# The last batch's second shared product moved behind the routed tiles, and the conditional tiles behind all

## The chip, the cores and the metric

The kernel runs on one core of one Trainium2 chip. The metric is the device time of one execution in microseconds (us). Times in the profile count from the first instruction of the span. The engines are called as in the profile: PE (TensorE, the matmuls) with its weight loads PEld, DVE (VectorE), ACT (ScalarE), POOL (GpSimd) and SP (SyncE, which here only issues transfers). A "q" behind an engine's name is its sequencer.

## The reference

Eight batches of 256 rows of 512 numbers (2048 rows, float32) pass through cross-attention and then a mixture of experts, each with a residual:

```python
x = x + xattn(layernorm(x), ctx, ctx)            # 32 heads of 16, 8 key/value groups, then @ Wfc.T + bfc
h = layernorm(x)
scores = softmax(h @ gate_weight.T)              # 8 experts
topk_w, topk_i = group_limited_topk(scores)      # 2 of 8 experts for each row
e = einsum(silu(h @ gate_w) * (h @ up_w), down_w)        # each expert, width 352
routed = sum over the two chosen experts of e * topk_w
shared = (silu(h @ sh_gate_w.T) * (h @ sh_up_w.T)) @ sh_down_w.T   # width 704, every row
x = x + routed + shared
```

The change touches `shared` of the last batch, in its second product, the one with `sh_down_w`.

## The kernel before, in words

The kernel has two parts. In the attention part PE goes through the 64 units of attention, and a planner (`Others`, with `Stage` objects that have a cost, a start and a due time) fills the gaps between them with the other work of each batch `b`: projections, `close(b)` (the product with Wfc, the residual in `acc`, the second layernorm), `router(b)` (the choice of experts, and the scattering of each row into a table `rows` in device memory, ordered by expert, with an indirect transfer from POOL) and `feed.pieces(b)` of the class `Shared`. `pieces(b)` is a generator. It makes first the products `gu` with the shared gate and up weights (L173) and from them `act`, then the second product `o` with the shared down weights (L193), one group of six products for each half (`q`) of the batch. DVE adds `acc` to it (L202) and SP writes the sum to `out` (L204). Every yielded piece is reckoned at 0.88 by the planner; `Shared.TOTAL` is their sum.

When attention is over, the pieces of the last batch (7) are handed as `tail` to `routed`. On PE the tail lies between attention and the routed tiles. The instruction order on PE, ACT, DVE and SP is that of the program text. SP's order at the handover is: weights of expert 0 (`up_weights`, `down_weights`, L365 and L368), rows of tiles 0 to 2 (`load`, L386), weights of experts 1 and 2, eight transfers `rows<-blank` which clear the ends of the experts' parts of the table (L536), the tail's two writes of `out`, and then what `run` issues. The tail is stepped to 0.8 of its cost, then tile 0 is transposed (`turn(0)`), then the tail is stepped to its end.

In the routed part a tile is 128 rows for one expert (or twice 64 rows for two experts, a "half" tile). 35 tiles are run: the first tile of each of the 8 experts, 24 further ones, and 3 half tiles at positions 12, 19 and 26. `run` is a software pipeline. In iteration `n` it issues the load of the rows of tile `n+2` and, at the start, the weights of the expert three tiles ahead, so the rows of tile 3 stand on SP behind the weights of expert 3. PE then does `turn` of tile `n+1` (four transpositions, `rx`, L397, copied by ACT), `up` of tile `n` (16 products `rg`, L429), `down` of tile `n-1` (6 products `ro`, L460) and `turn_act` of tile `n` (`ra`, L452). The result of `down` is weighted by DVE (`ry`, L471) and added to its rows of `out` in device memory by an indirect transfer of POOL that accumulates (L474). Each of these waits for the one before, since all write `out`. `last` does the last tile in smaller steps.

The second experts' weights of the half tiles are loaded into two tiles of their own, `wgu_2` and `wd_2` (`second`, L390 and L391).

How many tiles are needed depends on the data. `plan` works it out on the chip (`t_all`), and what the 35 tiles can't hold is done by `more`: every engine loads the value (L557) and branches (`tc.If`, L563). With these inputs nothing more is needed, so all engines only take the branch. `more` is called in iteration `MORE_AT`, 27.

Of the kernel before, what the change touches and what calls it, by code (L numbers as in the profile page):

```python
# [43 lines left out]
F32 = mybir.dt.float32  # L44
# [6 lines left out]
P = 128  # L51
# [20 lines left out]
N_HALF = N_EXP // 2  # L72
RUN_FULL, RUN_HALF = 24, 3
N_PLAN = N_FULL + N_HALF
MORE_AT = 27
W = 528
W_ID = D + N_EXP
EPS = 1e-5
# [6 lines left out]
@with_exitstack  # L85
def xattn_ffn(
    ctx: ExitStack,
    tc: tile.TileContext,
    x: bass.AP,
    ctxT: bass.AP,  # L90
    wq: bass.AP,
    wkv: bass.AP,
    wfc: bass.AP,
    bfc: bass.AP,
    wgate: bass.AP,
    wsg: bass.AP,
    wsd: bass.AP,
    wgu: bass.AP,
    wd: bass.AP,
    out: bass.AP,  # L100
):
    nc = tc.nc

    ctx.enter_context(tc.manual_schedule(engines={ENG.PE, ENG.Activation, ENG.DVE, ENG.SP}))

    keep = ctx.enter_context(tc.tile_pool(name="keep", bufs=1))
    dram = ctx.enter_context(tc.tile_pool(name="dram", bufs=1, space=bass.MemoryType.DRAM))
    ps_m = ctx.enter_context(tc.tile_pool(name="ps_m", bufs=3, space=PSUM))
    right = ctx.enter_context(ExitStack())
    left = ctx.enter_context(ExitStack())  # L110

    ident = keep.tile([P, P], F32, name="ident")
    make_identity(nc, ident)


    t_exp = keep.tile([P, N_PLAN], I32, name="t_exp")
    t_row = keep.tile([P, N_PLAN], I32, name="t_row")
    t_one = keep.tile([P, N_PLAN, N_EXP], F32, name="t_one")
    t_all = keep.tile([P, 1], I32, name="t_all")

    t_end = keep.tile([P, N_EXP], I32, name="t_end")

    blank = dram.tile([R, W], F32, name="blank")
    rows = dram.tile([N_EXP * S_R + P, W], F32, name="rows")

    feed = Shared(right, tc, ps_m, wsg, wsd, out)
    tail = attention(
        left, tc, ps_m, feed, x, ctxT, wq, wkv, wfc, bfc, wgate, out, ident,
        rows, t_exp, t_row, t_one, t_all, t_end, blank,
    )  # L130
    left.close()
    routed(ctx, tc, ps_m, wgu, wd, ident, rows, t_exp, t_row, t_one, t_all, t_end, blank, out, tail, right)


class Shared:


    TOTAL = (11 + 2 * 3) * 2 * 0.88

    def __init__(self, ph, tc, ps_m, wsg, wsd, out):  # L140
        self.nc, self.ps_m, self.wsg, self.wsd, self.out = tc.nc, ps_m, wsg, wsd, out
        wp = ph.enter_context(tc.tile_pool(name="wsh", bufs=1, side="right"))
        self.sums = ph.enter_context(tc.tile_pool(name="sums", bufs=2, side="right"))
        act = ph.enter_context(tc.tile_pool(name="act", bufs=1, side="right"))
        self.work = ph.enter_context(tc.tile_pool(name="sg", bufs=2, side="right"))

        self.gu = {
            k: wp.tile([P, NC, 2 * n if n == P else P], F32, name=f"gu_w{k}") for k, n in SCH
        }
        self.down = wp.tile([P, len(SCH), D], F32, name="down")  # L150
        self.hT, self.acc = {}, {}

        self.act = act.tile([P, len(SCH), S], F32, name="act")
        self.nc.gpsimd.memset(self.act[SCH[0][1] :, SCH[0][0]], 0.0)
# [10 lines left out]
    def pieces(self, b):  # L165
        nc, ps_m = self.nc, self.ps_m
        hT = self.hT.pop(b)
        act = self.act
        for k, n in SCH:
            ps = ps_m.tile([P, 2, S], F32, tag="m", name=f"gu{b}_{k}")  # L170
            for i in range(2 if n == P else 1):
                for c in range(NC):
                    nc.tensor.matmul(  # L173
                        ps[:, i],
                        lhsT=self.gu[k][:, c, i * P : (i + 1) * P],
                        rhs=hT[:, c],
                        start=(c == 0),
                        stop=(c == NC - 1),
                    )
                    if c == 1 or (c == NC - 1 and i == 0 and n == P):  # L180
                        yield 0.88, True, 0
            gate, up = ps[:n, 0], ps[:, 1] if n == P else ps[n:, 0]

            sg = self.work.tile([P, S], F32, tag="sg", name=f"sg{b}_{k}")
            nc.scalar.activation(sg[:n], gate, AF.Tanh, scale=0.5)
            nc.vector.scalar_tensor_tensor(sg[:n], sg[:n], 1.0, gate, ALU.add, ALU.mult)
            nc.vector.scalar_tensor_tensor(act[:n, k], sg[:n], 0.5, up, ALU.mult, ALU.mult)
            yield 0.88, False, 0
        acc = self.acc.pop(b)
        for q in range(QC):  # L190
            ps = ps_m.tile([P, D], F32, tag="m", name=f"o{b}_{q}")
            for i, (k, n) in enumerate(SCH):
                nc.tensor.matmul(  # L193
                    ps,
                    lhsT=act[:, k, q * P : (q + 1) * P],
                    rhs=self.down[:, k],
                    start=(i == 0),
                    stop=(i == len(SCH) - 1),
                )
                if i < len(SCH) - 1:  # L200
                    yield 0.88, True, 0
            nc.vector.tensor_add(acc[q], ps, acc[q])  # L202
            t0 = (b * QC + q) * P
            nc.sync.dma_start(self.out[t0 : t0 + P, :], acc[q])  # L204
            yield 0.88, False, 0
# [133 lines left out]
    tc.add_to_no_dep_group("rows", dma)  # L339


def routed(ctx, tc, ps_m, wgu, wd, ident, rows, t_exp, t_row, t_one, t_all, t_end, blank, out, tail, right):

# [34 lines left out]
    def load(i):  # L380
# [3 lines left out]
        for p in range(0, P, step):  # L384
            first = i * S_R if k < 0 else value(t_row, k, ENG.SP, N_EXP * S_R, p)
            nc.sync.dma_start(xs[i][p : p + step], rows[bass.ds(first, step), :])  # L386

    def second(i):
        e = value(t_exp, i - N_EXP, ENG.SP, N_EXP - 1, R)
        nc.sync.dma_start(wgu_2, wgu[bass.ds(e, 1)].rearrange("o p c f -> p (o c) f"))  # L390
        nc.sync.dma_start(wd_2, wd[bass.ds(e, 1)].rearrange("o p c d -> p (o c) d"))  # L391

    def turn(i):
# [12 lines left out]
            nc.vector.tensor_mul(wt, row[:, D : D + N_EXP], t_one[:, i - N_EXP])  # L406
            nc.vector.tensor_reduce(w1s[i], wt, AX.X, ALU.add)
        ids[i] = []
        for part, _ in halves(i, None, None):
            to = place(early, [P, 1], f"id{part.start}", f"rid{i}_{part.start}", 6, I32)  # L410
            to = to[: part.stop - part.start]
            nc.vector.tensor_copy(to, row[part, W_ID : W_ID + 1].bitcast(I32))
            ids[i].append(to)

    def halves(i, w, w_2):

        if i < N_EXP + N_FULL:
            return [(slice(0, P), w)]
        return [(slice(0, R), w), (slice(R, P), w_2)]

    def of_expert(i):
        exps[i] = i if i < N_EXP else value(t_exp, i - N_EXP, ENG.PE, N_EXP - 1)
# [1 line left out]
    def product(dst, i, cols):  # L424

        for c in range(NC):
            w = wgu_all[:, bass.ds(exps[i], 1), c, cols].rearrange("p o f -> p (o f)")
            for part, w in halves(i, w, wgu_2[:, c, cols]):
                nc.tensor.matmul(  # L429
                    dst[part],  # L430
                    lhsT=xTs[i][:, c, part],
                    rhs=w,
                    start=(c == 0),
                    stop=(c == NC - 1),
                )
# [20 lines left out]

    def down_chunk(o, i, fc, fn):
        w = wd_all[:fn, bass.ds(exps[i], 1), fc].rearrange("p o d -> p (o d)")
        for part, w in halves(i, w, wd_2[:fn, fc]):
            nc.tensor.matmul(  # L460
                o[part],
                lhsT=aTs[i][:fn, fc, part],
# [5 lines left out]
    def add_up(o, i):  # L468
# [1 line left out]
        y = place(work, [P, D], "y", f"ry{i}", 3)  # L470
        nc.vector.tensor_scalar(y, o, w1s.pop(i), None, ALU.mult)  # L471

        for to, (part, _) in zip(ids.pop(i), halves(i, None, None)):
            nc.gpsimd.indirect_dma_start(  # L474
                out=out,
                out_offset=bass.IndirectOffsetOnAxis(ap=to, axis=0),
# [57 lines left out]
    for e in range(N_EXP):  # L534
        to = value(t_end, e, ENG.SP, N_EXP * S_R)
        alone(tc, nc.sync.dma_start(rows[bass.ds(to, R), :], blank).ins)  # L536
    while tail.cost < 0.8 * tail.total:
        tail.step()
    turn(0)
    while not tail.over:  # L540
# [5 lines left out]
    others = ctx.enter_context(  # L546
        tc.tile_pool(name="others", bufs=1, side="right", reuse_waits="tile")
    )

    wgu_2 = others.tile([P, NC, 2 * F], F32, name="wgu_2")  # L550
    wd_2 = others.tile([P, len(FCH), D], F32, name="wd_2")

    def more():

        nonlocal spare
# [18 lines left out]
    def run(tiles):  # L574

        halfs = [n for n, i in enumerate(tiles) if i >= N_EXP + N_FULL]
        seconds = [0 if len(tiles) < N_EXP else N_EXP - 3, *(n + 3 for n in halfs)]
        for n, i in enumerate(tiles):
            if 3 <= n + 2 < len(tiles):
                load(tiles[n + 2])  # L580
            if i + 3 < N_EXP:
                up_weights(i + 3)
                down_weights(i + 3)
            for k, at in zip(halfs, seconds):
                if at == n:
                    second(tiles[k])
            if n + 1 == len(tiles):
                last(i, tiles[n - 1])
                break
            turn(tiles[n + 1])  # L590
            up(i)
            if n > 0:
                down(tiles[n - 1])
            turn_act(i)
            if n == MORE_AT:
                more()

    full = [N_EXP + k for k in range(N_FULL)]
    half = [N_EXP + N_FULL + k for k in range(N_HALF)]
# [6 lines left out]
def attention(  # L606
# [368 lines left out]
    def close(b):  # L975
# [7 lines left out]
        for qc in range(QC):  # L983
            ps = ps_m.tile([P, D], F32, tag="m", name=f"fc{b}_{qc}")
            for c in range(NC):
# [7 lines left out]
                if c < NC - 1:  # L993
                    yield 0.88, True, 0
            nc.vector.tensor_add(acc[qc], ps, acc[qc])
            moments(mv, acc[qc], qc, f"f{b}")
            if qc == 0:
                yield 0.88, False, 0
# [284 lines left out]
    def closed(b):  # L1283
        end = UNITS * (b + 1)
        if b + DEEP in gates:
# [11 lines left out]
            )  # L1297
        )
        shared.append(
            others.add(feed.pieces(b), feed.TOTAL, end + 6, end + 16.5, cl, *shared[-1:])  # L1300
        )

    def transfers():
# [122 lines left out]
```

## Time and profile before

| | |
|---|---|
| median of 3 runs | 945.8 us (943.48 to 947.02) |
| the profiled execution | 944.63 us, of which 942.9 us are the span from the first to the last instruction |
| PE busy | 923.3 us (98%) |
| DVE, ACT, POOL busy | 454.4, 202.7, 134.1 us |
| PE's granted clock over the span | 0.997 |
| shared second products `o` (L193), 8 batches | 192 instructions, 90.3 us busy |
| routed up products `rg` (L429) | 552 instructions, 169.3 us busy |
| SP's queue | 66.43 MB, 21.9% of 16 DMA engines' span |
| POOL's queue of indirect transfers | 17.83 MB, 8.9% |

A float32 product shows as two matmul instructions. The start of a group in the timeline is the start of its first instruction; the ends of matmuls are modelled and overlap the next start, so that the time of a group on PE is read from one start to the next. The table of 40 slices has one digit for each 23.6 us. The handover from attention to the routed tiles lies in slices 27 and 28.

### The profile page before, as it was taken

To read this page: it belongs to the slowest core of one execution; us is meant where nothing else is said; L and a number is where in the kernel's file an instruction comes from. 1 tells how busy PE (TensorE), PEld (TensorE's weight loads), DVE (VectorE), ACT (ScalarE), POOL (GpSimd) and SP (SyncE) were. 2 spreads that over 40 slices of the span, in tenths; PEclk is the share of its full clock that TensorE was granted. 3 is DMA by queue.
4 is the path that set the end of the run, shared out by engine and by line. 5 is a ranking of instruction groups with operands and counts; after the bars stand their busy time and mean duration, and the time that the engine had idled before them with its cause. 6 is when DMAs were issued, how large, how long until landed. Compare 5 with 4: busy or idle time off the path is not lost. (4 is left out here: it accounts for less than half of the span.)

```text
span 942.9 us, 12985 instructions
## 1 busy us (share of the span) xinstructions
PE 923.3 (98%) x5005; PEld 545.0 (58%) x5005; DVE 454.4 (48%) x1028; ACT 202.7 (21%) x257; POOL 134.1 (14%) x171
## 2 busy tenths in 40 slices
PE   9999999999999999999999999999999999999995
PEld 8775566546445555664654645785566555564563
DVE  4554857466756766554775645371222222222222
ACT  1224123323222232222232231101111111111110
POOL 4000100201101101100121021020121121121211
PEclk9999999999999999999999999999999999999998
DMA  6367610201102111002011011079963353533322
GB/s 223 84 199 227 172 36 2 83 6 34 47 13 81 47 24 46 27 27 45 24 47 46 1 48 45 23 273 382 396 162 73 83 147 63 149 69 68 68 34 34
DMA packets 37904, 86.23 MB, mean 91 GB/s; under 512 B 6289, under 2 KB 14737, under 8 KB 35921
## 3 DMA queue, kind: packets, MB, share of 16 engines
q1 hardware_dynamic: 29152, 66.43, 21.9%
q0 software_dynamic: 7648, 17.83, 8.9%
q10 hardware_dynamic: 1040, 1.12, 0.4%
q8 instruction: 42, 0.69, 0.3%
q14 instruction: 22, 0.17, 0.1%
HBM read 54.99 MB, written 25.93 MB: 86 GB/s over the span
## 5 line engine op out<-in xcount | busy, mean ns | idle before, releaser
L904 DVE TENSOR_REDUCE nm<-s 128x8 f32<-128x2048 f32 x64 | 146.5, 2289 | 86.5 <-PE s L895 82.3
L429 PE MATMUL rg<-wgu_all,rxT 128*128 (+2 forms) x552 | 169.3, 460 | 0.0
L936 ACT ACTIVATE ex<-s 128x2048 f32<-128x2048 f32 x64 | 120.1, 1877 | 225.8 <-PE s L928 216.1
L173 PE MATMUL gu<-hT,gu_w 128*128 128x256 f32 x704 | 166.6, 385 | 0.0
L173 PEld LDWEIGHTS gu<-hT,gu_w 128*128 128x128 f32 x704 | 129.1, 190 | 41.0 <-issue 24.6
L429 PEld LDWEIGHTS rg<-wgu_all,rxT 128*128 128x128 f32 (+1 forms) x552 | 99.6, 185 | 53.6 <-issue 6.9
L460 PE MATMUL ro<-wd_all,raT 128*128 (+5 forms) x210 | 96.5, 594 | 0.0
L474 POOL DMA_INDIRECT y<-ry,rid x38 | 58.4, 1537 | 253.3 <-DVE ry L471 140.7
L193 PE MATMUL o<-down,act 128*128 128x512 f32 x192 | 90.3, 603 | 0.3 <-DVE q L334 0.3
L446 DVE TENSOR_TENSOR ract<-rg,rsg 128x352 f32<-128x352 f32 x34 | 17.8, 524 | 139.6 <-PE rg L429 139.6
L928 PE MATMUL s<-qT,kT 17*128 17x512 f32 x512 | 73.0, 640 | 2.0 <-DVE nm L904 1.9
L895 PE MATMUL s<-kT,qT 16*128 16x256 f32 x1024 | 73.4, 400 | 1.5 <-ACT ex L936 0.8
L895 PEld LDWEIGHTS s<-kT,qT 16*128 16x128 f32 x1024 | 46.3, 184 | 30.9 <-ACT ex L936 14.1
L460 PEld LDWEIGHTS ro<-wd_all,raT 128*128 128x128 f32 (+3 forms) x210 | 38.4, 186 | 42.9 <-issue 36.2
L861 PE MATMUL pq<-xT,wq_sb 128*128 128x256 f32 x256 | 61.2, 386 | 0.5 <-DVE acc L202 0.3
L947 PE MATMUL av<-ex,v 128*32 128x512 f32 x512 | 61.5, 598 | 0.0
L986 PE MATMUL fc<-wfc_sb,o 128*128 128x512 f32 x128 | 60.9, 603 | 0.1
L471 DVE TENSOR_SCALAR ry<-ro,rw 128x512 f32<-128x512 f32 x35 | 26.3, 750 | 71.9 <-PE ro L460 71.9
L399 ACT COPY rxT<-rx 128x512 f32<-128x512 f32 x35 | 20.5, 585 | 187.4 <-PE rx L397 187.4
L1111 POOL DMA_INDIRECT rows<-lnf,idx x32 | 31.6, 988 | 200.6 <-DVE idx L1105 189.7
L193 PEld LDWEIGHTS o<-down,act 128*128 128x128 f32 x192 | 33.9, 190 | 40.6 <-issue 39.3
L861 PEld LDWEIGHTS pq<-xT,wq_sb 128*128 128x128 f32 x256 | 46.6, 190 | 14.5 <-issue 6.0
(183 smaller groups left out, 723.6 us busy)
## 6 DMA issues: line engine op xcount, KB each, us to landing
wgu_all<-wgu SPq DMA_DIRECT2D x8, 1408.0 KB
xs<-rows SPq DMA_DIRECT2D x32, 264.0 KB
wd_all<-wd SPq DMA_DIRECT2D x8, 768.0 KB
wgu<-wgu SPq DMA_DIRECT2D x3, 1408.0 KB
cT<-ctxT SPq DMA_DIRECT2D x8, 512.0 KB
acc<-x SPq DMA_DIRECT2D x16, 256.0 KB
y<-acc SPq DMA_DIRECT2D x16, 256.0 KB
x<-x SPq DMA_DIRECT2D x14, 256.0 KB
```

The lines of the kernel that those rows point to most:

```text
L173: nc.tensor.matmul(ps[:, i], lhsT=self.gu[k][:, c, i * P : (i + 1) * P], rhs=hT[:, c], start=(c == 0), stop=(c == NC - 1),)
L193: nc.tensor.matmul(ps, lhsT=act[:, k, q * P : (q + 1) * P], rhs=self.down[:, k], start=(i == 0), stop=(i == len(SCH) - 1),)
L429: nc.tensor.matmul(dst[part], lhsT=xTs[i][:, c, part], rhs=w, start=(c == 0), stop=(c == NC - 1),)
L460: nc.tensor.matmul(o[part], lhsT=aTs[i][:fn, fc, part], rhs=w, start=(fc == 0), stop=(fc == len(FCH) - 1),)
L474: nc.gpsimd.indirect_dma_start(out=out, out_offset=bass.IndirectOffsetOnAxis(ap=to, axis=0), in_=y[part], in_offset=None, compute_op=ALU.add,)
L861: nc.tensor.matmul(ps[:, i], lhsT=wq_sb[:, c, part], rhs=xT[:, c], start=(c == 0), stop=(c == NC - 1),)
L895: nc.tensor.matmul(ps[:, r, j], lhsT=qT[band, G, j0 + j, qc * P : (qc + 1) * P], rhs=kT[band, G], start=True, stop=True,)
L904: nc.vector.tensor_reduce(nms[b, G, j0][:, qc], ps, AX.X, ALU.max, negate=True)
L928: nc.tensor.matmul(ps[:, r], lhsT=kT[band, G, kc * P : (kc + 1) * P], rhs=qT[band, G, j0 : j0 + 2], start=True, stop=True,)
L936: nc.scalar.activation(ex, ps, AF.Exp, scale=HD**-0.5)
L947: nc.tensor.matmul(av[32 * r : 32 * r + 32], lhsT=vs[b % DEEP][:, kc, 4 * G + r], rhs=ex[:, r], start=(kc == 0), stop=(kc == QC - 1),)
L986: nc.tensor.matmul(ps, lhsT=o[:, c, qc * P : (qc + 1) * P], rhs=wfc_sb[:, c], start=(c == 0), stop=(c == NC - 1),)
```

## The change

`pieces` of the last batch ends after the first product. `act` is written to a new table `kept` in device memory by SP, in the place where the tail's two writes of `out` stood. `close` of the last batch writes `acc` (input plus attention) to `out` at once. After the last tile the two halves of batch 7 are read back from `out`, which by then has the routed parts added, the second product is made from `kept` and the down weights (both loaded again in iteration 28, into the buffer of the half tiles' second weights, which becomes one tile `two`), added to them, and written. `more` comes behind that. The tail stops two pieces before its end for `turn(0)`, and in iteration 0 `turn(1)` stands behind `up(0)` instead of before it.

```diff
 class Shared:
-    TOTAL = (11 + 2 * 3) * 2 * 0.88
+    UP = 11 * 2 * 0.88
+    TOTAL = UP + 2 * 3 * 2 * 0.88
...
             yield 0.88, False, 0
+        if b == B - 1:
+            nc.sync.dma_start(self.kept, act)
+            return
         acc = self.acc.pop(b)
...
+    def two(a, m, b, n):
+        t = others.tile([P, len(SCH) * (D + S)], F32, tag="two", name="two")
+        return (
+            t[:, : a * m].rearrange("p (a m) -> p a m", m=m),
+            t[:, a * m : a * m + b * n].rearrange("p (b n) -> p b n", n=n),
+        )
...
     def second(i):
         e = value(t_exp, i - N_EXP, ENG.SP, N_EXP - 1, R)
+        seconds[i] = wgu_2, wd_2 = two(NC, 2 * F, len(FCH), D)
...
-    while tail.cost < 0.8 * tail.total:
+    while tail.cost < tail.total - 2 * 0.88:
         tail.step()
     turn(0)
...
-            turn(tiles[n + 1])
+            if n == halfs[-1] + 2:
+                down_sh, act_sh = two(len(SCH), D, len(SCH), S)
+                nc.sync.dma_start(down_sh, wsd)
+                nc.sync.dma_start(act_sh, kept)
+            if n > 0:
+                turn(tiles[n + 1])
             up(i)
             if n > 0:
                 down(tiles[n - 1])
+            else:
+                turn(tiles[n + 1])
             turn_act(i)
-            if n == MORE_AT:
-                more()
+
+        sums = []
+        for q in range(QC):
+            t0 = ((B - 1) * QC + q) * P
+            to = out[t0 : t0 + P, :]
+            sums.append((to, work.tile([P, D], F32, tag=f"sum{q}", bufs=1, name=f"sum{q}")))
+            nc.sync.dma_start(sums[q][1], to)
+        for q, (to, y) in enumerate(sums):
+            ps = ps_m.tile([P, D], F32, tag="m", name=f"o{B - 1}_{q}")
+            for i in range(len(SCH)):
+                nc.tensor.matmul(
+                    ps,
+                    lhsT=act_sh[:, i, q * P : (q + 1) * P],
+                    rhs=down_sh[:, i],
+                    start=(i == 0),
+                    stop=(i == len(SCH) - 1),
+                )
+            nc.vector.tensor_add(y, ps, y)
+            nc.sync.dma_start(to, y)
+        more()
...
             nc.vector.tensor_add(acc[qc], ps, acc[qc])
+            if b == B - 1:
+                nc.sync.dma_start(out[(b * QC + qc) * P : (b * QC + qc + 1) * P, :], acc[qc])
             moments(mv, acc[qc], qc, f"f{b}")
...
-            others.add(feed.pieces(b), feed.TOTAL, end + 6, end + 16.5, cl, *shared[-1:])
+            others.add(
+                feed.pieces(b), feed.UP if b == B - 1 else feed.TOTAL, end + 6, end + 16.5, cl, *shared[-1:]
+            )
```

## The prediction

> **What bounds the kernel now.** I read the page first, then four answers of the trace: the chain of waits, TensorE's (PE's) waits, the timeline around the handover from the attention part to the routed part, and the timeline of the start and the end. The page says that PE is busy nearly throughout:
>
> ```profile
> span 942.9 us, 12985 instructions
> PE 923.3 (98%) x5005; PEld 545.0 (58%) x5005; DVE 454.4 (48%) x1028; ACT 202.7 (21%) x257; POOL 134.1 (14%) x171
> DMA  6367610201102111002011011079963353533322
> ```
>
> So moving PE work changes the time only by what it leaves uncovered. The DMA row shows one place where PE isn't alone: slices 27 to 29 (about 613 to 684 us) are the loading of the routed weights. By windows:
>
> ```profile
> 628.00:649.00 21.00, 21.00 (x74) 13.02 (x73) 5.22 (x20) 3.68 (x6) 0.00 (x0) 1.00 0.92 360
> 649.00:659.00 10.00, 9.31 (x35) 5.39 (x33) 1.98 (x7) 1.05 (x2) 0.00 (x0) 1.00 1.00 386
> ```
>
> The last three columns are granted clock, DMA share and GB/s: PE and the DMA engines are full at the same time. Here the change takes PE work away and takes hardly a byte from the DMA. The sync queue's (SP's) issues in that stretch, and PE's timeline:
>
> ```profile
> 634.85 11.61 SPq L536 DMA_DIRECT2D rows<-blank  x8
> 646.55 1.00 SPq L204 DMA_DIRECT2D y<-acc  x2
> 647.61 0.45 SPq L365 DMA_DIRECT2D wgu_all<-wgu  x1
> 648.10 0.43 SPq L368 DMA_DIRECT2D wd_all<-wd  x1
> 648.78 0.33 SPq L386 DMA_DIRECT2D xs<-rows  x1
> ```
> ```profile
> 633.71 5.31 PE L193 MATMUL o<-down,act 128*128 128x512 f32 x12
> 638.86 0.60 PE L397 MATMUL rx<-ident,xs 128*128 128x128 f32 x4
> 639.30 5.32 PE L193 MATMUL o<-down,act 128*128 128x512 f32 x12
> 658.61 0.49 PE L452 MATMUL ra<-ident,ract 128*128 128x128 f32 x3
> 659.16 0.63 PE L397 MATMUL rx<-ident,xs 128*128 128x128 f32 x4
> ```
>
> The last line is the transposition of tile 3. Its rows are the `xs<-rows` load issued at 648.78; that load's sixteen completion increments arrive from 656.09 to 659.02, 0.14 us before PE starts on it. Before the change PE meets this load just as it lands. That is the centre of my prediction.
>
> **Part 1: the second product leaves the handover.** Two groups of 12 instructions, 5.15 us each by the starts above (633.71 to 638.86), so PE is 10.3 us earlier if nothing stops it. Follow it: the first product ends at 633.9; tile 0's rows land at 632.85, so its transposition, now two pieces earlier, starts at 633.0 instead of 632.1; with the rest of the pieces the first product ends at 635.1. Then `up(0)` 4.73, transposition of tile 1 0.44, 0.25 for the activation (the wait was 0.69, and the swapped transposition, 0.44, now lies in it), `turn_act` 0.38, tile 2 0.44, `up(1)` 4.73, `down(0)` 2.58, `turn_act` 0.38: PE stands before tile 3 at 649.0, ten microseconds early. Tiles 1 and 2 (landed by 634.7) and the weights of experts 0 to 2 (landed by 645.9, expert 1's by 640.7) don't stop it.
>
> Tile 3's load can't come earlier. On SP it stands behind the eight `blank` transfers and expert 3's weights, in the new program too, and the queue moves its bytes in order: from 628 us 768 + 3x264 + 2x2176 + 8x132 + 512 + 2176 + 264 = 9920 KB. The change takes out the 512 KB of `y<-acc` (now sent when `close` has added, when the DMA is nearly idle) and puts in `kept<-act`, 768 KB. The page gives that queue 21.9% of the span for 66.43 MB, 3.1 us per MB: 0.26 MB more is +0.8 us. Tile 0's scatter-add, formerly issued at 659.84 and so behind this load, is now issued near 650; its queue takes 8.9% for 17.83 MB, 4.7 us per MB, so its 0.26 MB costs up to 1.2 us of the same engines. Bounds for tile 3's landing: 656.1 (all sixteen parts as the earliest) plus 0.8, up to 659.02 + 0.8 + 1.2. I take 659.9, nearest to the measured landing with half of these additions, so PE starts tile 3 at 660.05 against 659.16: **+0.9 us** (range -2.0 to +2.0). The 10.3 us removed are a wait of 11 us. Behind it nothing is late: tile 4's rows landed at 664.96, and PE wants them 8 us after tile 3.
>
> **Part 2: the clock after that wait.** The trace has both ends of such a pause (timeline of the start, then the windows of the end):
>
> ```profile
> 1.81 4.45 PE L1217 MATMUL warm<-ident 128*128 128x128 f32 x20 [1.81 <-POOL ident masks.py:199]
> 7.83 1.95 PE L805 MATMUL pkv<-wkv_sb,cT 128*128 128x128 f32 x16
> ```
> ```profile
> 938.00:943.00 5.00, 0.00 (x0) 0.00 (x0) 0.00 (x0) 0.00 (x0) 0.00 (x0) 0.50 0.11 20
> ```
>
> Twenty products of 128 columns take 4.45 us at the start, later sixteen take 1.95: 0.22 against 0.11 us each, so PE runs at half speed for its first 4.2 us. And after its last matmul (932.6) the granted clock falls to 0.50 (at 937.8, 5.2 us later). A pause of 11 us therefore costs half of about 4.2 us: **+2.1 us**, between 1.7 and 3.4 for where the change of clock falls.
>
> The Trainium skill ("TensorE: Matmul & The Clock Gate", "What's actually happening") speaks against the change at this place: it has the array halve its clock after an idle window of about 3.4 us and regain it after as long a busy one. By that the price would be an estimated 1.7 us in place of 2.1, and a wait of 4 us would already pay it, which no row here shows.
>
> **Part 3: the conditional tiles leave tile 27.**
>
> ```profile
> PE rx L397 <- PEq L563: 1.9, 1, 1.9
> ```
>
> PE waits once for its branch, 1.9 us with nothing beside it; the path is PE's from there to the end. **-1.9 us.** At the new place the branch lies behind all of PE's work; its cost belongs to the end.
>
> **Part 4: small things.** `act_sh` and `down_sh` are 2.3 MB on SP at iteration 28, about 6 us at 386 GB/s; the next `xs` load queues behind them and is wanted two iterations (16 us) later: nothing. If that cover were gone, up to 6 us. The wait of `kept<-act` on SP holds up expert 3's weights and tile 3's load behind it, but `act` is done near 636.5 and SP gets there at 646.5: nothing. The one tile for both second weights changes no order. The early writes of batch 7's `acc` make SP wait near 584, but its next instruction waits for batch 6 until 608 anyway: nothing.
>
> **Part 5: the end.** Now:
>
> ```profile
> 932.65 0.75 DVE L471 TENSOR_SCALAR ry<-ro,rw 128x512 f32<-128x512 f32 x1 [1.44 <-PE ro L460]
> 934.56 1.55 POOL L474 DMA_INDIRECT y<-ry,rid  x1 [4.03 <-DMA y<-ry,rid]
> ```
> ```profile
> 934.34 1.77 POOLq L1422
> ```
>
> PE ends at 932.6, the last scatter-add lands at 939.17, and the program ends 3.7 us later: 0.8 for SP's closing waits, then GpSimd's (POOL's) drain until 942.1, then 0.8 of handshake. After the change (same clock face) PE goes on with the product: 2x5.15 = 10.3 us, to 942.9. Meanwhile SP waits for the scatter, reads the rows back from 939.25 (`acc<-x`, the same size, took 2.8 us to land: 942.05, the second half 942.6), so the read is hidden, with 0.3 us to spare; behind SP's wait for it stand only the two writes. POOL, which has its own branch behind the last scatter, waits there for its landing and then 1.4 us (the `INC_SWDGE_SEM` of L563), to 940.7, and holds up nobody. Last come the addition, 0.69 (the `acc<-o,acc` form), the write, 2.1 (`y<-acc` at 608.36 and 616.32 landed after 2.02 and 2.16), 0.2 of the branch's semaphores on SP, 0.8 of closing and 0.8 of handshake, POOL's drain being over by then: 942.9 + 0.15 + 0.69 + 0.1 + 2.1 + 0.2 + 1.6 = 947.7, against 942.9: **+4.8 us**. Bounds: 4.5 without the branch, 6.9 if the drain follows the landing as it does now. So the product is not free behind the tiles: of its 10.3 us, 5.5 fall into time in which PE was already done.
>
> **Sum.** +0.9 + 2.1 - 1.9 + 4.8 = +5.9 us. The profiled execution took 944.63 us (942.9 of span and 1.7 around it), so it becomes 950.5. It lay 1.2 us below the median of the three runs; from the median: 951.7 us.
>
> **Rivals.** (a) *The freed PE time is kept* (faster). If tile 3's rows were in place by 649.0, PE would gain the ten microseconds and no clock would fall: -10.0 - 1.9 + 4.8 = -7.1, 938.7 us. It decides by one thing: each microsecond that tile 3's load lands before 659.0 is one gained, and the change is even where it lands at about 656 with the clock up, or 654 with it down. For it speaks that PE is 98% busy; against it the DMA share of 0.92 and 1.00 and the 9920 KB ahead of the load. Chance 0.05. (b) *The load lands early within its own spread* (no change). The sixteen parts lay 2.9 us apart; if the slowest engine doesn't lag in the new order, tile 3 starts at about 657.3: -1.9 + 1.9 - 1.9 + 4.8 = +2.9, 948.7 us. The spread of expert 1's load was 1.6, so a lag of 2.9 isn't the rule. Chance 0.27. (c) *A worse end*, drain and read-back included: +6.9 instead of 4.8, 953.8 us; counted with the forecast.
>
> **How the numbers follow.** The forecast, rows of tile 3 waited for, clock halved, end exposed, has 0.68. About 0.5% (4.7 us) is what a measurement of this kernel can tell from no change; +5.9 is over it, +2.9 within it. Low end: -2.0 + 1.7 - 1.9 + 4.5 = +2.3, or 948.1, opened to 947.5 for a shorter end; high end: +2.0 + 3.4 - 1.9 + 6.9 = +10.4, or 956.2.
>
> **What would show it.** Right: no `o` matmul before tile 0; PE idle for about 10 us before the transposition of tile 3, released by `xs<-rows`; matmuls at twice their spacing for some 4 us behind it; `rx(4)` some 3 us later than 667.3; no wait on L563 among the tiles; PE's last matmul about 10 us after the last tile's, and the span's end some 5 us behind that. Wrong: tile 3 transposed near 650, or the read-back landing after the product.

## The result, and the profile after

The changed kernel took 952.8 us (median of 5 runs, 951.49 to 954.48) against 946.97 us (5 runs) of the kernel before, run beside it: a ratio of 1.0068 with a 95% interval of 1.0046 to 1.0091, or +6.4 us (4.4 to 8.6); the two medians lie 5.8 us apart. The profiled execution took 951.49 us, 1.8 of them outside the span. Its page, first, busy and clock lines:

```profile
span 949.7 us, 12997 instructions
PE 925.4 (97%) x5005; PEld 546.4 (58%) x5005; DVE 454.1 (48%) x1028; ACT 202.6 (21%) x257; POOL 134.2 (14%) x171
...
PEclk9999999999999999999999999997999999999999
```

PE executes as many matmuls as before (x5005), is busy 2.1 us longer, and the clock row has one slice at 7, slice 28 (counted from 1), in the handover. The span is 6.8 us longer, and PE is busy for 2.1 of them; in the rest it stands. PE's waits (us in total, times, longest):

```profile
PE rx L423 <- DMA xs<-rows: 11.8, 2, 11.0
```

PE's timeline at the place (start, us; the bracket is the idle time before and its releaser):

```profile
649.37 0.49 PE L478 MATMUL ra<-ident,ract 128*128 128x128 f32 x3
660.89 1.08 PE L423 MATMUL rx<-ident,xs 128*128 128x128 f32 x4 [11.03 <-DMA xs<-rows]
661.77 6.52 PE L455 MATMUL rg<-wgu_all,rxT 128*128 128x352 f32 x16
668.13 2.74 PE L486 MATMUL ro<-wd_all,raT 128*128 128x512 f32 x6
...
671.03 0.60 PE L423 MATMUL rx<-ident,xs 128*128 128x128 f32 x4
```

PE is ready for tile 3 at 649.7 and stands until 660.89: the ten microseconds of moved products are gone into one wait on the load. The next four transpositions take 1.08 us where those of tile 4 take 0.60, and the sixteen `rg` products need 6.36 us from start to start instead of 4.73. The windows show why (last three columns: granted clock, DMA share, GB/s):

```profile
649.80:654.80 5.00, 0.07 (x1) 0.00 (x0) 1.05 (x3) 0.00 (x0) 1.61 (x1) 1.00 0.96 337
654.80:660.90 6.10, 0.01 (x1) 0.04 (x1) 0.12 (x2) 0.00 (x0) 0.00 (x0) 0.50 1.04 364
660.90:665.00 4.10, 4.10 (x10) 2.83 (x11) 0.10 (x2) 0.58 (x1) 0.00 (x0) 0.50 1.02 424
665.00:671.00 6.00, 6.00 (x20) 3.33 (x20) 0.62 (x2) 0.46 (x1) 0.00 (x0) 1.00 1.02 426
```

The clock falls at 654.80, 4.9 us after PE's last work ended, and comes back at 665.04, with PE already working for 4.1 us. All this time the DMA engines are full. At the other end of the program (first from the chain of work that ended last, then the timeline of SP and DVE):

```profile
934.10 10.32 PE o L634 x24
```
```profile
940.32 0.81 SPq L630 DMA_DIRECT2D sum<-y  x2
...
942.99 0.69 DVE L641 TENSOR_TENSOR sum<-o,sum 128x512 f32<-128x512 f32 x1 [8.09 <-DMA sum<-y]
943.70 1.80 SPq L642 DMA_DIRECT2D y<-sum  x2
944.44 0.69 DVE L641 TENSOR_TENSOR sum<-o,sum 128x512 f32<-128x512 f32 x1 [0.77 <-PE o L634]
```

The product runs until 944.4 without a gap; the first addition is released by the read-back (landed 942.89), the second, the one that counts, by PE. The write of the second half lands at 947.56, and the span ends at 949.7.

The starts of the same instructions in both traces divide the 6.8 us: +0.55 in the attention part, where the change touches nothing; +1.18 in the start of tile 3; +2.03 from there to tile 4's transposition; -2.27 from there to the last tile's last matmul; +5.29 from that to the end.

### The profile page after: what moved, and what is told of

Same layout as the page of the kernel before. It is cut to its first block, busy times and chain, and to the rows that moved or that the text cites. A ratio compares the mean times of both kernels' runs of the same rounds, so it can differ in the third digit from the quotient of the medians.

```text
span 949.7 us, 12997 instructions
## 1 busy us (share of the span) xinstructions
PE 925.4 (97%) x5005; PEld 546.4 (58%) x5005; DVE 454.1 (48%) x1028; ACT 202.6 (21%) x257; POOL 134.2 (14%) x171
## 4 chain that ended last, share of the span: by engine, by line
PE 89%; DVE 5%; DMA 3%; SPq 1%; ACT 1%; issue 1%; POOL 0%; ACTq 0%; DVEq 0%; POOLq 0%
PE rg L455 17%; PE gu L180 14%; PE ro L486 10%; PE o L204 8%; PE s L942 7%; PE s L975 7%; PE fc L1033 6%; PE av L994 5%; PE pq L908 5%; PE rx L423 2%; DMA xs<-rows 2%; DVE nm L951 1%; PE pkv L852 1%; PE ra L478 1%; PE pkv L841 1%; PE o L634 1%
## 5 line engine op out<-in xcount | busy, mean ns | idle before, releaser
L204 PE MATMUL o<-down,act 128*128 128x512 f32 x168 | 79.6, 604 | 0.3 <-DVE q L345 0.3
L204 PEld LDWEIGHTS o<-down,act 128*128 128x128 f32 x168 | 29.4, 190 | 35.8 <-issue 34.5
```

The costliest lines, as they stand in the source:

```text
L204: nc.tensor.matmul(ps, lhsT=act[:, k, q * P : (q + 1) * P], rhs=self.down[:, k], start=(i == 0), stop=(i == len(SCH) - 1),)
```

## The experiments

Each kernel was run beside the kernel before on the same chip; ratios are to that kernel, whose medians were 945.5 to 946.1 us there (22 to 32 runs). The changed kernel was not run again beside them, so it is compared through its own ratio, 1.0068 (1.0046 to 1.0091), and through the traces. My theory: the time of the handover is set by the transfers, so PE work removed there becomes a wait, and the wait has a price of its own, the clock. The rival: PE's work counts, and something added by the change ate the gain.

**1. Only the removal.** `no_second` is the kernel before without the second product of batch 7, and with nothing put in its place.

```diff
         for q in range(QC):
+            if b < B - 1:
                 ps = ps_m.tile([P, D], F32, tag="m", name=f"o{b}_{q}")
                 ...                       # product and addition, as before
...
-    while tail.cost < 0.8 * tail.total:
+    while tail.cost < 20 * 0.88:
```

> The kernel before, with the second shared product of batch 7 left out altogether (its part of the output is missing; everything else as before, and act of batch 7 is made but not used). Theory: 10.3 us of PE work less at the handover gain nothing, because PE then waits some 10 us for tile 3's rows, and the clock falls in that wait: tile 3 starts 0 to 1.5 us later than before (scatter of tile 0 now runs beside the loads), plus 2.1 us of half clock: 947 + 2.1 to 3.6 = 949 to 950.6 us, slower with less work. Rival (the handover is bound by PE): 10.3 us less, 936.7 us.

Measured: 949.9 us, ratio 1.0040 (1.0023 to 1.0056). With 10.3 us less PE work the kernel is slower. PE's timeline shows the same wait and the same slow products:

```profile
659.46 1.09 PE L398 MATMUL rx<-ident,xs 128*128 128x128 f32 x4 [9.93 <-DMA xs<-rows]
660.34 7.24 PE L430 MATMUL rg<-wgu_all,rxT 128*128 128x352 f32 x16
```

The clock was at 0.50 from 651.40 to 665.05, 5.6 us of that with PE at work, and a second time for 3.41 us behind the branch in iteration 27, where it stays up in the trace of before. Of the 4.7 us between the two spans (947.6 and 942.9), the later start of tile 3 makes 0.3 (659.46 against 659.16), the half clock behind it 2.8 and the second fall 1.7. So neither `kept` nor the new end is needed for the loss at the handover; the rival falls.

**2. Only the clock.** `dull` is the changed kernel with forty products of the identity with itself before the transposition of tile 3, whose results nobody reads. They keep PE occupied inside the wait.

```diff
+            if n == 2:
+                dull = ps_m.tile([P, NC, P], F32, tag="m", name="dull")
+                for k in range(40):
+                    nc.tensor.matmul(dull[:, k % 4], lhsT=ident, rhs=ident, start=True, stop=True)
             if n > 0:
                 turn(tiles[n + 1])
```

> The changed kernel, with 40 products of 128 columns (ident by ident, some 8.8 us at full clock) that nobody reads put before the transposition of tile 3, that is into the wait. Theory (the clock falls in the wait and costs 2.05 us behind it): the wait shrinks to some 2 us, tile 3 starts at the same time, granted clock 1.00 throughout, 2.0 us less: 950.7 us. Rival (the matmuls behind the wait are slow for another reason, or the time is taken back later): 952.8 us; if the wait is shorter in other runs the products would even cost time.

Measured: 950.3 us, ratio 1.0045 (1.0029 to 1.0061), where the changed kernel has 1.0068: about 2.2 us less, but the two intervals overlap. PE's timeline:

```profile
650.22 9.10 PE L619 MATMUL dull<-ident 128*128 128x128 f32 x80
661.03 0.63 PE L423 MATMUL rx<-ident,xs 128*128 128x128 f32 x4 [1.71 <-DMA xs<-rows]
661.49 4.90 PE L455 MATMUL rg<-wgu_all,rxT 128*128 128x352 f32 x16
...
669.13 0.60 PE L423 MATMUL rx<-ident,xs 128*128 128x128 f32 x4
```

Tile 3 starts at the same time (661.03 against 660.89), but its transpositions and products have their full speed, the clock stays at 1.00, and tile 4 starts 1.9 us sooner (669.13 against 671.03). So the trace shows the 2 us of the clock by themselves, apart from the wait. They last to PE's last matmul (942.5 against 944.4), but not to the end of this execution, whose span is 950.0 us against 949.7:

```profile
943.46 1.34 DVE L645 TENSOR_TENSOR sum<-o,sum 128x512 f32<-128x512 f32 x2 [10.47 <-DMA sum<-y]
```

Its last scatter-add took 6.0 us to land instead of 4.8, and the rows read back behind it arrived at 944.02, 1.5 us after the end of the product. Here the read-back, not PE, set the end.

**3. Fewer bytes ahead of the load.** `act_stays` keeps `act` of batch 7 in on-chip memory to the end: the 768 KB of `kept<-act` ahead of tile 3's rows, and the reload, are gone.

```diff
-    kept = dram.tile([P, len(SCH), S], F32, name="kept")
+    kept = keep.tile([P, len(SCH), S], F32, name="act")
...
-            nc.sync.dma_start(self.kept, act)
             return
...
-                nc.sync.dma_start(act_sh, kept)
```

> The changed kernel, with act of batch 7 kept in SBUF until the end instead of written to kept and loaded again; the order of everything else as in the changed kernel. Theory (tile 3's rows wait for the bytes ahead of them): 768 KB less in front of them, so they land 2.0 to 2.6 us earlier, the wait falls from 11.0 to about 8.7 us, the clock still falls: 2.0 to 2.6 us less than the changed kernel, ratio to before about 1.0045. Rival (the wait is set by the issue on SP, each instruction waiting for an earlier landing): 0.5 us less at most.

Measured: 948.4 us, ratio 1.0028 (1.0012 to 1.0043), 3.8 us less than the changed kernel, by the ratios and by the spans (945.9 against 949.7) alike; the intervals don't overlap. PE's timeline:

```profile
657.29 1.09 PE L421 MATMUL rx<-ident,xs 128*128 128x128 f32 x4 [7.61 <-DMA xs<-rows]
```

The wait is 3.4 us shorter for 0.77 MB less: 4.4 us per MB at this place. The clock still falls (half from 651.81 to 662.05, 4.8 us of it with PE at work), so its price stays. Of the 3.8 us, 3.3 are there when tile 4 starts (667.73 against 671.03), the rest arises at the end. I had expected 2.0 to 2.6.

**4. The load out of the queue.** `tile3_early` only issues the rows of tile 3 before the tail's rest, ahead of `kept` and of expert 3's weights.

```diff
     turn(0)
+    load(3)
     while not tail.over:
...
-            if 3 <= n + 2 < len(tiles):
+            if 4 <= n + 2 < len(tiles):
                 load(tiles[n + 2])
```

> The changed kernel, with only tile 3's load moved ahead of kept<-act and expert 3's weights (still behind the blank transfers); tile 4's and later loads as they were. Theory (each tile's rows stand behind the weights ahead of them, so one load moved ahead only hands the wait to the next): tile 3 waits 2 to 3 us (its rows land near 651.8), tile 4 waits 6 to 8 us (landing near 667, wanted near 660): together 9 to 10 us, span some 1 to 2 us under the changed kernel's 949.7. Rival (tile 3's load alone is late): one wait of 2 to 3 us, span 938 to 940.

Measured: 950.6 us, one run. PE's timeline:

```profile
652.06 0.77 PE L423 MATMUL rx<-ident,xs 128*128 128x128 f32 x4 [2.60 <-DMA xs<-rows]
...
667.48 1.08 PE L423 MATMUL rx<-ident,xs 128*128 128x128 f32 x4 [5.46 <-DMA xs<-rows]
```

The wait of 11.0 is split into 2.6 for tile 3 and 5.5 for tile 4, each with a half clock behind it (3.41 and 6.83 us): nearly all of the gain at tile 3 is lost one tile on. It isn't one load that is late for an early PE, it is the queue.

`rows_early` loads the rows of every tile one iteration sooner, and puts the eight blank transfers, which had to go somewhere, at iteration 3:

```diff
-    for e in range(N_EXP):
-        ...                               # rows<-blank, now in blanks()
...
     turn(0)
+    load(3)
...
-            if 3 <= n + 2 < len(tiles):
-                load(tiles[n + 2])
+            if 4 <= n + 3 < len(tiles):
+                load(tiles[n + 3])
             ...
+            if n == 3:
+                blanks()
```

> The changed kernel, with the load of tile 3's rows put ahead of kept<-act and of expert 3's weights, each later tile's rows loaded three iterations ahead instead of two (so ahead of the weights of their own iteration), and the eight blank transfers moved from the handover to iteration 3. Theory (queue order: PE waits for tile 3's rows because some 10 MB stand ahead of them): tile 3's rows land near 647.5, tile 4's near 656.5 (wanted at 658), expert 3's weights near 655 (wanted at 658); the wait of 11.0 us and the half clock behind it (2.05 us) go, so 13 us less than the changed kernel, about 939.7 us, and 7 us (0.8%) less than the kernel before. Rival 1 (the DMA's throughput is the bound, not the order): PE meets expert 3's or 4's weights instead and waits 5 to 8 us there, so 945 to 948 us. Rival 2 (the wait is worth nothing since something later waits as well): no change against the changed kernel, 952.8 us.

Measured: 944.9 us, ratio 0.9994 (0.9978 to 1.0009), where I had expected about 0.992. Tiles 3 and 4 now start at 649.64 and 657.71 without a wait, as expected. But the lost time came back at a place of my own making. SP's issues and PE's timeline:

```profile
669.78 8.82 SPq L563 DMA_DIRECT2D rows<-blank  x8
680.69 0.35 SPq L401 DMA_DIRECT2D xs<-rows  x1
```
```profile
685.76 1.09 PE L423 MATMUL rx<-ident,xs 128*128 128x128 f32 x4 [3.65 <-DMA xs<-rows]
```

The blank transfers write to the table from which the rows are read, so SP waits for the rows of tile 6 (landed 669.77) before it issues them, and then issues them for 8.8 us. Tile 7's load stands behind all that, is 3.65 us late, and the clock is at half for 6.83 us.

`rows_and_act` keeps `act` on the chip as in `act_stays`, puts the blank transfers back at the handover, but behind the early load of tile 3, and issues the expert weights one iteration later.

```diff
     turn(0)
+    load(3)
+    for e in range(N_EXP):
+        ...                               # rows<-blank
     while not tail.over:
...
-            if i + 3 < N_EXP:
-                up_weights(i + 3)
-                down_weights(i + 3)
+            if 3 <= i + 2 < N_EXP:
+                up_weights(i + 2)
+                down_weights(i + 2)
```

> The changed kernel with two things changed: act of batch 7 stays in SBUF until the end (no kept table, so 768 KB less on SP at the handover and again at iteration 28), and the rows of tiles 3 and later are loaded three iterations ahead, before the blank transfers (tile 3) or before the weights of expert 3 (tile 4), while the weights are issued two iterations ahead. The blank transfers stand at the handover again, not in iteration 3 where rows_early had them and where they held up tile 7's rows (wait of 3.65 us, and the clock fell again). Theory (queue order at the handover is all that held the time): tile 3's rows land near 647.5, tile 4's near 652, expert 3's weights near 656 (wanted at 658), no wait above 1 us among the tiles, granted clock 1.00: 6.5 us less than rows_early, 938.4 us, ratio to before 0.9925. Rival (throughput of the DMA binds: the next load in line is late whatever the order): one wait of 3 us or more at tiles 3 to 8 and no better than 942 us.

Measured: 947.2 us, ratio 1.0016 (1.0004 to 1.0028), 9 us more than I had expected, through the same mistake. SP's issues:

```profile
647.60 8.29 SPq L564 DMA_DIRECT2D rows<-blank  x8
```

They wait for tile 3's rows (landed 647.59); while SP issues them (647.6 to 655.9) the DMA engines move 136 GB/s, against 319 in the 7.6 us before, and then tile 4's rows and expert 3's weights are both late (waits of 2.45 and 3.39 us, and 6.83 us of half clock).

**5. The branch and the end.** `more_last` is the kernel before with the branch moved behind the last tile, and nothing else.

```diff
             turn_act(i)
-            if n == MORE_AT:
-                more()
+        more()
```

> The kernel before, with the conditional tiles alone moved from iteration 27 behind the last tile. PE's wait of 1.9 us at L563 goes in every theory. Theory 1 (GpSimd's closing drain takes 5.8 us from its last instruction, as both traces have it: 936.1 to 942.1 before, 942.0 to 947.8 after; behind the last scatter its branch now waits for the landing at 939.2 and 1.5 us for INC_SWDGE_SEM): the end comes 4.7 us later, in sum 2.8 us more than before, 949.8 us. Theory 2 (the drain only waits for the landing, as my prediction had it): the end costs some 0.6 us, in sum 1.3 us less, 945.7 us.

Measured: 947.2 us, ratio 1.0006 (0.9994 to 1.0019; the medians lie 1.7 us apart): between the two expectations, and its profiled span is 945.6, 2.7 us longer than that of before. POOL's closing drains in its trace (ns of the shortest, median and longest, then the starts of the first and the last, in us):

```profile
L1421 POOLq DRAIN  x3: 51/107/5778, 939.0 to 945.3; - x3
```

POOL waits at its branch until the last scatter has landed (937.1), spends 1.57 us there, and only then begins a drain of 5.78 us, which ends the program; SP had been done at 940.1. So the drain follows POOL's last instruction, not the landing. In the changed kernel it runs from 942.0 to 947.8, 1.1 us before SP is done: hidden, narrowly.

`more_27` is the changed kernel with the branch back in iteration 27.

```diff
             turn_act(i)
+            if n == 27:
+                more()
...
-        more()
```

> The changed kernel with the conditional tiles back in iteration 27. Theory: PE waits 1.9 us for its branch there; at the end SP loses the semaphores of the branch (0.5 us behind the last landing) and GpSimd's drain ends earlier but was off the path: 1.4 us more than the changed kernel, ratio to before about 1.008. Rival (the drain or the branch at the end costs as much as the branch in the middle, as more_last suggests for the kernel before): no difference, 1.0065.

Measured: 955.2 us, ratio 1.0104 (1.0088 to 1.0120), about 3.4 us more than the changed kernel's (2.6 by the spans, 952.3 against 949.7). I had expected 1.4. PE's timeline:

```profile
876.83 0.96 PE L423 MATMUL rx<-ident,xs 128*128 128x128 f32 x4 [2.14 <-PEq L585]
```

A wait of about 1.9 was expected. Behind it the clock was at half from 876.98 to 880.39, half of 3.41 or 1.7 us, which the trace of before does not have after its wait of 1.91 at the same branch. From the start of tile 4 to PE's last matmul this execution takes 4.3 us more than that of the changed kernel, where the trace of before takes 2.3 more: the branch among the tiles costs PE 2.3 us, or 4.3 where the clock falls with it. At the end, where the branch no longer stands, 1.3 us come back (4.0 us from the last matmul to the end of the span, against 5.3).

**6. A version that beats both.** `blanks_later` is `rows_early` with the blank transfers at iteration 4 instead of 3; `blanks_later_act` is that with `act` kept on the chip, as in `act_stays`; `before_reordered` puts the order of `blanks_later` (rows one iteration sooner, blank transfers at iteration 4) into the kernel before, which shows what the order is worth without the moved product.

```diff
 # blanks_later, against rows_early
-            if n == 3:
+            if n == 4:
                 blanks()
 # blanks_later_act, against blanks_later: the edit of act_stays
-    kept = dram.tile([P, len(SCH), S], F32, name="kept")
+    kept = keep.tile([P, len(SCH), S], F32, name="act")
...
 # before_reordered, against the kernel before: the edits of rows_early, with n == 4
     turn(0)
+    load(3)
...
```

> rows_early with the eight blank transfers one iteration later (4 instead of 3), that is behind the load of tile 7's rows and expert 7's weights, so that their wait for earlier loads of rows holds up nothing that is wanted soon. Theory (order on SP at the handover and behind it is what binds): no wait above 1.2 us at tiles 0 to 8, the clock doesn't fall, and the 3.65 us wait and the 3.4 us lost at half clock of rows_early go: 6.5 us less than rows_early's 944.9, ratio to before about 0.993. Rival (another load is late wherever the order is changed, since the DMA is nearly full until 690): again one wait of 3 us or more at tiles 7 to 10, ratio 0.997 to 1.000.

> blanks_later with act of batch 7 kept in SBUF until the end (no kept table). Theory: in blanks_later no load is late, so 768 KB less at the handover change nothing that PE waits for: the same time as blanks_later within 0.1%. Rival (the handover's bytes still bind): up to 2 us less.

> The kernel before with the same reordering as blanks_later (tile 3's rows first, rows three iterations ahead, blank transfers in iteration 4), the second product where it was. Theory: PE had no wait at the handover to lose, so no change: ratio 1.000 (within 0.2%). Rival (the reordering is a gain by itself, not the cover that the move needs): 0.995 or less.

Measured: `blanks_later` 944.0 us, ratio 0.9981 (0.9967 to 0.9996); `blanks_later_act` 938.4 us, **0.9921 (0.9906 to 0.9937)**; `before_reordered` 945.4 us, 0.9989 (0.9978 to 1.0001). For `blanks_later` I had expected 0.993, and no long wait. It keeps one before tile 8, whose load stands behind the blank transfers (SP 679.0 to 687.3), and a half clock of 3.41 us behind it:

```profile
693.31 1.08 PE L423 MATMUL rx<-ident,xs 128*128 128x128 f32 x4 [2.27 <-DMA xs<-rows]
```

`blanks_later_act` loses both: with 768 KB less, tile 7's rows land at 674.36 instead of 678.84, the blank transfers start at 674.5 and tile 8's rows are there at 688.83, before PE wants them (690.34). I had expected it to equal `blanks_later`, or gain 2 us at most: it gained 5.5, of which the wait and the half clock make 4.0. Its page and PE's timeline:

```profile
span 936.2 us, 12991 instructions
...
PEclk9999999999999999999999999999999999999999
```
```profile
649.95 0.60 PE L421 MATMUL rx<-ident,xs 128*128 128x128 f32 x4
...
658.03 0.60 PE L421 MATMUL rx<-ident,xs 128*128 128x128 f32 x4
```

Tile 3 starts 9.2 us before its time in the kernel before, with no wait, and the clock never falls until the end. This is the prediction's rival (a), priced at -7.1 us and measured at -7.5 (-6.0 to -8.9). `before_reordered` shows that the order alone gives about 1 us (-0.1 to 2.1): in the kernel before, the product that the change moves covers the loads, and there is little to gain from sooner ones. In its profiled execution the clock fell behind the branch, too:

```profile
873.82 0.63 PE L397 MATMUL rx<-ident,xs 128*128 128x128 f32 x4 [1.85 <-PEq L566]
```

That cost it 3.41 us at half clock after a wait of 1.85, though the longer wait of 1.91 in the trace of before cost none (the last section has the reason).

## Why the prediction was right

The forecast was +5.9 us; the profiled executions differ by 6.8, and the timed runs by 6.4 (4.4 to 8.6). The mechanism of each of its four steps is in the traces. That the sum comes so close is in part luck: 0.55 of the 6.8 us arose where the change does nothing, and the size of the clock's step depends on a moment that nothing in the program sets. By its steps:

- *Tile 3's start*, +0.9: measured +1.2 beyond the shift that PE brings from the attention part. The reason given, that the load can't come earlier, holds: in the experiment without added bytes but without the product, too, PE waited (9.93 us). The size came from prices per MB averaged over the queues, 3.1 and 4.7; at this place 0.77 MB were worth 3.4 us, 4.4 per MB. The load's sixteen parts arrived from 659.02 to 660.76, closer together than the 2.9 us of before, as rival (b) asked, but none early: the first came 2.9 us later than before, so the earlier start of rival (b) did not happen. Its reason, that a lag of 2.9 isn't the rule, was a wrong reading: in the trace of before the loads beside tile 3's lag alike (the two of expert 3's weights 3.2 and 2.9, tile 4's rows 2.9).
- *The half clock*, +2.1: measured +2.03 in the trace, and 1.9 us at tile 4 in `dull`. A like fall behind a like wait cost 2.8 us in the traces of `no_second` and `more_27` (5.6 us of work at half clock) and 2.4 in that of `act_stays` (4.8), all within the range of 1.7 to 3.4 that the prediction gave. To have met 2.03 was luck.
- *The branch*, -1.9: measured -2.27 in the traces over the whole stretch in which it lies, and 4.3 us on PE in `more_27`, where the clock falls with it. The step priced the wait and left out the clock, though the step before it had just priced one. In the profiled execution of before the clock didn't fall there; in most of its other runs it seems to. Of the 32 runs of before beside `more_last`, ten have a granted clock of 0.997, as the profiled one, and take 944.4 us in the mean, and nineteen have 0.995 and take 946.3. A fall of 3.41 us would take 0.002 off the granted clock and add 1.7 us. The runs of `more_last` take 947.1 us in the mean, 2.7 more than the former, as in the traces, and 0.8 more than the latter. Where in these runs the clock fell, no trace shows.
- *The small things*, 0: the weights loaded again in iteration 28 and SP's wait for `act` made no wait on PE among the tiles. But the 768 KB of `kept` weren't free at the handover: they were in the sum, as bytes, and `act_stays`, which has none of them, gives back 3.8 of the 6.4 us, 3.3 of them at the handover (512 KB of writes stood in that place before).
- *The end*, +4.8: measured +5.29. The write took 2.40 us to land instead of 2.1, the branch's semaphores on SP 0.45 instead of 0.2. The read-back's second half had landed 0.9 us before the end of the product, where 0.3 was forecast; in `dull` it landed 1.5 us after it, so that the read is not always hidden. The upper bound of 6.9 rested on a drain that follows the landing; it follows POOL's last instruction, and it was hidden by 1.1 us.
- The other 0.55 us arose in the attention part, 0.14 at its start and the rest by 76.7 us; the change has no hand in it, and runs of one kernel lie up to 7 us apart.

Rival (a) was priced rightly and refused rightly: it needs the rows of tile 3 by 649, and the changed kernel has no means to bring them. It became true with three edits that the change didn't contain.

## What to carry to other kernels

PE work that stands in front of a stage whose transfers fill the DMA engines is cover for these transfers: taking it away buys nothing, and costs a clock fall, until the bytes or their order change too. When a load is moved ahead, follow the queue past it: what must wait for that load (here a transfer that overwrites the table it reads) and what stands behind the waiting one; `rows_early` and `rows_and_act` lost their gain there. A move that looks free in bytes should be checked for a copy that can simply stay on the chip.

## What was not expected of the hardware

Half-clock stretches in the middle of the program came in lengths of 3.41, 6.83, 10.24 and 13.65 us only, multiples of 3.41. More than that: within each of the thirteen traces all changes of the clock lie whole multiples of 3.41 us apart, and where this grid lies against the program differs from run to run. The Trainium skill ("TensorE: Matmul & The Clock Gate", "What's actually happening") explains such a grid by a free-running activity window of 3413 ns, which these lengths agree with.

The grid also says what decides whether a short wait costs the clock. In these traces it is the part of the wait that lies between two marks of the grid. The clock fell, each time at the mark, behind every stretch between two marks in which PE, with the clock up, stood for 2.13 us or more by the modelled ends (23 of the 25 falls, those after PE's last matmul included), and behind none in which it stood for 1.76 or less; between these, two stretches of 1.85 and 1.86 us ended in a fall and one of 1.96 didn't. In `before_reordered` the whole wait of 1.85 us (871.97 to 873.82) lies between the marks 871.36 and 874.77, and the clock fell at 874.77. In the trace of before a mark at 872.93 (nineteen steps ahead of the fall at 937.78) cuts the wait of 1.91 us into 1.58 and 0.33:

```profile
873.26 0.63 PE L397 MATMUL rx<-ident,xs 128*128 128x128 f32 x4 [1.91 <-PEq L563]
```

The skill's table in that section asks for at least one idle window before the clock falls; here the clock fell after waits of 1.85, 2.14, 2.27 and 2.60 us, and the measurement decides: a pause of 2 us can cost 1.7 us more, by where it falls on the grid.

GpSimd's closing drain took 5.78 us in each of the nine traces in which GpSimd's branch is its last work, and began when that branch had ended.
